# Four fused convolution layers with a woven state-space scan: the scan's inputs formed half a tile earlier, the products of the step preparation moved to other slots, the output sums two slots later

## The chip, the cores and the metric

One NeuronCore of a Trainium2 chip runs the whole program in one launch. The metric is device time in microseconds; three runs of the kernel before gave a median of 21075.38 us (21060.88 to 21089.58). A further run, taken with the hardware profiler, is the one that the profile and the trace describe: 21033.39 us, of which the instructions span 21031.6 us.

Engines are named as in the profile: PE is the matmul engine (PEld its weight loads), DVE the vector engine, ACT the scalar engine, POOL the GpSimd engine, SP the engine whose queue issues nearly all DMAs. Each works through its own list of instructions in the order in which the program gives them; semaphores hold an instruction until what it reads or overwrites is ready.

## The reference, cut to what matters

```python
# x: (4, 128, 128, 128) float32
x = x + _L0_conv_ref(_gn(x), ...)   # deformable 3x3 convolution (bilinear gathers)
x = x + _L1_conv_ref(_gn(x), ...)   # dilated 5x7 convolution and two 1x1 layers
x = x + _L2_conv_ref(_gn(x), ...)   # layer norm, depthwise convolutions, state-space scan, gate, layer norm
x = x + _L3_conv_ref(_gn(x), ...)   # 3x3 convolution and a Laplacian of the channel sum
```

The change lies in the scan of layer 2, which runs in four directions k over every image (by rows and by columns, each forwards and backwards):

```python
dts = einsum('bkrl,kdr->bkdl', dts, dt_w)
A = -exp(A_logs).reshape(K, C, 16)
delta = softplus(dts + dt_b[None, :, :, None])
def step(h, inp):
    u, d, b, c = inp                       # one position l
    dA = exp(d[..., None] * A)
    h = h * dA + (d * u)[..., None] * b[:, :, None, :]
    y = einsum('bkcn,bkn->bkc', h, c)
    return (h, y)
```

So each of 128 channels carries 16 states; each state is decayed by exp(delta·A), gets delta·u·B as its input, and the 16 states weighted by C are summed into y.

## The kernel before

**Blocks, tiles, slots.** `scan` works through 512 blocks: 4 images, 4 directions in the order k = 0, 1, 3, 2, and 32 blocks of 512 positions each. k = 0 and 1 are forward blocks, 3 and 2 are backward ones (`back`). A block t has 16 slots n = 4·j + g, with j the tile and g the place in it. A tile is an array `h` of 128 partitions x 4 x 512, which holds 4 of the 16 states of every channel. In each slot DVE runs one `tensor_tensor_scan` over 512 positions (L1071), 8192 in all.

**What a tile needs.**
- `states_up(t, j)` (L925): a PE product of B and `u` into the PSUM bank `dub`.
- `inputs(t, j, engine)` (L931): `h = du * dub`, one instruction over 128 x 2048. On DVE it reads `dub` from PSUM. In plain blocks (below) the tile j = 3 is formed by POOL instead, from `bb`, which a DMA brings.
- `decay` (L952): ACT computes exp(delta·A) into a bank `pa`, one for each slot. There are two such banks, and a third (`bank(3)`) in the stretches where the work beside the scan leaves it free. `decays(at)` keeps the list one or two decays ahead of the scan.
- After its four scans, `carry_on` and `outputs` (L989, L996) save the last column and multiply `h` by C, on POOL in plain blocks and on DVE in the others; `sums` (L966) adds the four states on PE into the bank `yacc`, and `finish` (L981) copies that bank out when a block is complete.

**The preparation of a later block.** `prepare(t + 2)` (L854) is a generator, and a slot from 1 to 15 makes one step of it. It computes delta = softplus(...) and delta·u in these instructions: product `pdt` (L866), its two evictions `e` and `above` on ACT (L871, L873), `exp` (L875), 1 + e (L878), in forward blocks the product `pxbc` (L882) and its eviction `bc` (L888), `ln` (L884), a subtraction (L890), four products into `psum` (L898), the eviction `steps` (L904), and on POOL delta·u (L908). `spread_steps`, `spread_products`, `spread_inputs` and `spread_outputs` bring the results, spread over partitions, back by DMAs on SP's queue, one block before their use.

**One bank for four kinds of product.** `pdt`, `pxbc`, `psum` and `dub` all have `tag="dub"` in a pool with one buffer for it. So each such product waits until the reader of the one before it is done: ACT's evictions for the first three, DVE's `inputs` for `dub`.

**Two kinds of block.** While layer 0 of a later image runs beside the scan, its gathers keep POOL busy; `c["by"]` is then DVE, and DVE does all four `inputs` and all `outputs`. I call these gather blocks. The other blocks are plain: POOL does `outputs` and the fourth `inputs`.

**What sets the order.** `together` runs the scan as the main list and takes steps of the work beside it (the layers of the images before and after) after each slot, by a fixed share. `keep_order` then fixes each engine's list in the order of emission. So the program's text is the order, on each engine.

**The slots of the shared bank before.** In slot 2 stands `pdt`, in slot 3 `e` and `above` and then `states_up` of tile 1; at the start of slot 4 `inputs` of tile 1. In slot 6 stands `pxbc` (forward blocks), in slot 7 `bc` and then `states_up` of tile 2; at the start of slot 8 its `inputs`. In plain blocks `psum` stands in slot 11, `steps` in 13, the POOL product in 14 and `states_up` of the next block's tile 0 in 15; in gather blocks `psum` in 9, `steps` in 10, `states_up` of tile 3 in 11, and again the next tile 0 in 15. `sums` of tile j stands in the second slot of tile j + 2.

The loop's core, as it stands:

```python
if ("h", j) not in c:
    inputs(t, j, nc.vector)
...
if g == 3 and then[0] < len(seq) and not (then[1] == NG - 1 and c["by"] is nc.gpsimd):
    states_up(*then)
```

Of the kernel before, what the change touches and what calls it, by code (L numbers as in the profile page):

```python
# [10 lines left out]
F32 = mybir.dt.float32  # L11
# [101 lines left out]
def conv_preact_kernel(ctx: ExitStack, tc: tile.TileContext, a: dict, nb: int):  # L113
# [20 lines left out]
    def store(dst, src, after=3, of=None):  # L134

        waiting.append([after, of, dst, src])
# [61 lines left out]
    def slots(n):  # L198
        for _ in range(n):
            yield None  # L200
# [617 lines left out]
    def scan(pull):  # L818
# [34 lines left out]

        def prepare(t, early=False):  # L854
# [3 lines left out]
            if (st["b"], k) not in carries:  # L858
                carries[st["b"], k] = carry = small.tile([P, NST], F32, name="carry")
                nc.vector.memset(carry, 0.0)  # L860
            c["carry"] = carries[st["b"], k]
            c["bc"] = st["bc"][k % 2][i, k // 2]
            u = c["u"]
            yield
            pdt = pss.tile([P, N], F32, name="pdt", tag="dub")
            nc.tensor.matmul(pdt, wd[:, k, :], u, start=True, stop=True)  # L866
            yield

# [5 lines left out]
            yield  # L874
            nc.scalar.activation(e, e, AF.Exp, scale=-1.0)  # L875
            yield
            one_e = sp.tile([P, N], F32, name="one_e", bufs=1)
            nc.scalar.activation(one_e, e, AF.Identity, bias=1.0)  # L878
            yield
            if not back:  # L880
                px = pss.tile([P, N], F32, name="pxbc", tag="dub")
                nc.tensor.matmul(px, xbc[:, k, :], u, start=True, stop=True)  # L882
# [3 lines left out]
            if not back:  # L886
                bc = sp.tile([4 * NST, N], F32, name="bc", bufs=1)
                nc.scalar.copy(bc, px[0 : 4 * NST])  # L888
                store(st["bc"][k][i].rearrange("d j s t -> (d j s) t"), bc)
# [9 lines left out]
            yield  # L899
            if not early:  # L900
                yield
# [3 lines left out]
            yield  # L905
            if early:
                yield
# [17 lines left out]
        def states_up(t, j):  # L925

            c = blocks[t]
            c["pb", j] = p = pss.tile([P, N], F32, name="dub", tag="dub")
            nc.tensor.matmul(p, xb[:, seq[t][1], j, :], c["u"], start=True, stop=True)  # L929
# [59 lines left out]
        def carry_on(t, j, engine=nc.gpsimd):  # L989

            end = 0 if seq[t][3] else N - 1
            h = blocks[t]["h", j]
            copy = nc.scalar.copy if engine is nc.scalar else engine.tensor_copy
            copy(blocks[t]["carry"][:, j * NG : (j + 1) * NG].unsqueeze(2), h[:, :, end : end + 1])  # L994
# [21 lines left out]
        states_up(0, 0)  # L1016
        decays(-1)
        slots = len(seq) * NST
        for t, (st, k, i, back) in enumerate(seq):
            c = blocks[t]  # L1020
            carry = c["carry"]
            on_vector = beside.get("busy") == "POOL"
            c["by"] = nc.vector if on_vector else nc.gpsimd
            more = prepare(t + 2, on_vector) if t + 2 < len(seq) else iter(())
            if t > 0:
                fetch(t + 3)
            for j in range(NG):
# [3 lines left out]
                if ("h", j) not in c:  # L1031
                    inputs(t, j, nc.vector)
                h = c["h", j]
                if t + 1 < len(seq) and j in (1, 2):
                    spread_steps(t + 1, j - 1)
                at = t * NST + j * NG
                decays(at)
                if j == 1 and t + 1 < len(seq):
                    spread_inputs(t + 1)
                if j == 2 and t + 1 < len(seq):  # L1040
                    spread_outputs(t + 1)
                if j == 3 and back:
                    c["before"] = load(sp, blk(st["y"][k % 2], i), [P, N], "before", bufs=1)
                for g in range(NG):
                    n = j * NG + g
                    if g == 1:
                        decays(at + 1)
                        if t + 1 < len(seq) and j == 3:
                            spread_steps(t + 1, 2)
                            spread_steps(t + 1, 3)  # L1050
                        if t + 1 < len(seq) and j == (2 if c["by"] is nc.gpsimd else 3):
                            spread_products(t + 1)
                        next(more, None)
                        if before[0] >= 0:
# [16 lines left out]
                    nc.vector.tensor_tensor_scan(o, f, o, carry[:, n : n + 1], ALU.mult, ALU.add)  # L1071
# [430 lines left out]
```

## Time and profile before

| | us |
|---|---|
| median of 3 runs | 21075.38 |
| profiled run | 21033.39 |
| its span | 21031.6 |
| DVE busy | 16808.6 (80%) |
| PE busy | 16025.3 (76%) |
| POOL busy | 15945.9 (76%) |
| ACT busy | 13477.7 (64%) |
| 8192 scans on DVE (L1071) | 9967.9, mean 1.266 |
| 1625 `inputs` on DVE (L936) | 3697.9, mean 2.276, and 1455.8 idle before them |
| 1692 `outputs` on POOL (L1000) | 7666.8, mean 4.531 |
| 8192 decays on ACT (L963) | 5551.9, mean 0.686 |
| DMA engines, moved | 4641.27 MB, 221 GB/s |

"Busy" is the time in which an engine works on an instruction of the program. "Idle before" is the time in which an engine waited for an instruction of a group, and the name after `<-` is what ended the wait. Until about 2300 us the first image's layers run alone, and after about 20690 us the last image's layer 3; between them the scan runs. The gathers (L445) run beside it in three stretches, about 3300 to 5450, 8500 to 10600 and 13600 to 15500 us, each recognised by POOL's time in L445; by the place of the 356 `outputs` that DVE makes, about 92 of the 512 blocks are gather blocks or hold part of one, and 420 are plain. Between the starts of two blocks lie 29.9 us in plain and 63.0 us in gather blocks, on average.

### The profile page before, as it was taken

To read this page: it belongs to the slowest core of one execution; us is meant where nothing else is said; L and a number is where in the kernel's file an instruction comes from. 1 tells how busy PE (TensorE), PEld (TensorE's weight loads), DVE (VectorE), ACT (ScalarE), POOL (GpSimd) and SP (SyncE) were. 2 spreads that over 40 slices of the span, in tenths; PEclk is the share of its full clock that TensorE was granted. 3 is DMA by queue.
4 is the path that set the end of the run, shared out by engine and by line. 5 is a ranking of instruction groups with operands and counts; after the bars stand their busy time and mean duration, and the time that the engine had idled before them with its cause. 6 is when DMAs were issued, how large, how long until landed. Compare 5 with 4: busy or idle time off the path is not lost.

```text
span 21031.6 us, 207094 instructions
## 1 busy us (share of the span) xinstructions
PE 16025.3 (76%) x58778; PEld 6877.1 (33%) x58778; DVE 16808.6 (80%) x14665; ACT 13477.7 (64%) x26854; POOL 15945.9 (76%) x9469
## 2 busy tenths in 40 slices
PE   4667776777877788777787887877777877777778
PEld 2444222444322223344432222344432222222223
DVE  1222588888998899888899889978889888999983
ACT  3444676676667776566667775666666766655563
POOL 3664477666788888767768888867768889999994
PEclk7788887988988889889898998989988988789899
DMA  7666568777756777777776696777776677555673
GB/s 234 192 193 184 162 202 282 249 256 250 245 192 204 213 236 246 246 249 249 254 237 196 202 251 217 262 241 252 256 242 204 205 208 216 185 185 191 196 220 123
DMA packets 2869274, 4641.27 MB, mean 221 GB/s; under 512 B 1088976, under 2 KB 1361944, under 8 KB 2791200
## 3 DMA queue, kind: packets, MB, share of 16 engines
q1 hardware_dynamic: 2499488, 3419.78, 50.9%
q0 software_dynamic: 368640, 1208.25, 18.2%
q8 instruction: 470, 7.70, 0.1%
q14 instruction: 676, 5.54, 0.1%
HBM read 3682.39 MB, written 874.52 MB: 217 GB/s over the span
## 4 chain that ended last, share of the span: by engine, by line
PE 24%; DVE 22%; ACT 14%; issue 13%; POOL 11%; DMA 8%; another core or an unknown queue 6%; SPq 2%; DVEq 0%; POOLq 0%; ACTq 0%
DVE h L1071 12%; DVE h L936 8%; POOL h L1000 7%; PE pst L481 6%; ACT g L458 5%; PE dub L929 3%; PE psum L898 3%; ACT pa L963 3%; PE yacc L974 2%; DMA du<-stepsd 2%; DMA delta<-stepsd 2%; PE p L1297 2%; POOL h L936 2%; PE acc L496 2%
## 5 line engine op out<-in xcount | busy, mean ns | idle before, releaser
L1071 DVE TENSOR_TENSOR_SCAN h<-pa,carry,h 128x512 f32<-128x512 f32 x8192 | 9967.9, 1266 | 474.7 <-ACT pa L963 236.8
L963 ACT ACTIVATE pa<-delta,neg_a 128x512 f32<-128x512 f32 x8192 | 5551.9, 686 | 3911.7 <-DVE h L1071 3239.1
L1000 POOL TENSOR_TENSOR h<-h,cb 128x2048 f32<-128x2048 f32 x1692 | 7666.8, 4531 | 136.5 <-POOL carry L994 0.6
L445 POOL DMA_INDIRECT g<-table,idx x4608 | 4814.8, 1045 | 2317.7 <-issue 1477.3
L936 DVE TENSOR_TENSOR h<-du,dub 128x2048 f32<-128x2048 f32 x1625 | 3697.9, 2276 | 1455.8 <-PE dub L929 1000.3
L481 PE MATMUL pst<-ident,g 128*128 128x128 f32 x18432 | 2705.1, 309 | 1641.8 <-ACT smp L490 1015.5
L481 PEld LDWEIGHTS pst<-ident,g 128*128 128x128 f32 x18432 | 2449.0, 161 | 2537.7 <-ACT smp L490 1405.8
L929 PE MATMUL dub<-u,xb_sb 128*128 128x512 f32 x3250 | 2046.4, 715 | 1478.8 <-ACT above L873 960.5
L974 PE MATMUL yacc<-h,gather_sb 128*32 128x512 f32 x16384 | 2468.7, 677 | 868.9 <-POOL h L1000 609.6
L458 ACT ACTIVATE g<-g,wt 128x128 f32<-128x128 f32 x9216 | 2869.2, 392 | 58.6 <-DMA g<-table,idx 47.7
L490 ACT COPY smp<-pst 128x512 f32<-128x512 f32 x1152 | 668.3, 580 | 2104.0 <-remote 1637.9
L936 POOL TENSOR_TENSOR h<-du,bb 128x2048 f32<-128x2048 f32 x423 | 1925.2, 4551 | 16.8 <-DMA du<-stepsd 15.8
L471 DVE TENSOR_TENSOR g<-g,wl 128x512 f32<-128x512 f32 x2304 | 1484.1, 669 | 171.1 <-DMA g<-table,idx 151.2
L994 POOL COPY carry<-h 128x4 f32<-128x4 f32 x1692 | 332.0, 196 | 1535.8 <-DVE h L1071 1479.3
L929 PEld LDWEIGHTS dub<-u,xb_sb 128*128 128x128 f32 x3250 | 580.8, 212 | 2522.8 <-ACT above L873 1377.2
L496 PE MATMUL acc<-smp,w_sb 128*128 128x512 f32 x2304 | 1318.9, 656 | 49.4 <-DVE x L503 36.2
L1297 PE MATMUL p<-xn,w_l_sb 128*128 128x508 f32 (+2 forms) x2304 | 1198.4, 638 | 1.8 <-ACT xn L1276 1.8
L503 DVE TENSOR_TENSOR x<-acc,xres 128x512 f32<-128x512 f32 x128 | 87.7, 685 | 1351.7 <-remote 478.9
L974 PEld LDWEIGHTS yacc<-h,gather_sb 128*32 128x32 f32 x16384 | 343.9, 113 | 2445.9 <-POOL h L1000 1075.9
L908 POOL TENSOR_TENSOR steps<-steps,u 128x512 f32<-128x512 f32 x512 | 658.7, 1286 | 326.1 <-ACT steps L904 313.6
L866 PE MATMUL pdt<-u,wd 128*128 128x512 f32 x1024 | 635.6, 706 | 278.0 <-DVE h L936 266.2
L750 PE MATMUL px<-win,convw_sb 128*128 128x508 f32 (+1 forms) x1536 | 806.8, 623 | 26.9 <-DMA win<-win 24.0
(171 smaller groups left out, 17914.0 us busy)
## 6 DMA issues: line engine op xcount, KB each, us to landing
cb<-bcd SPq DMA_DIRECT2D x512, 1024.0 KB
delta<-stepsd SPq DMA_DIRECT2D x2048, 256.0 KB
du<-stepsd SPq DMA_DIRECT2D x2048, 256.0 KB
stepsd<-steps SPq DMA_DIRECT2D x512, 512.0 KB
table<-gt SPq DMA_DIRECT2D x512, 256.0 KB
bb<-bcd SPq DMA_DIRECT2D x512, 256.0 KB
g<-table,idx POOLq DMA_INDIRECT x4608
u<-urow SPq DMA_DIRECT2D x256, 256.0 KB
```

The lines of the kernel that those rows point to most:

```text
L445: nc.gpsimd.indirect_dma_start(out=g[:, r].rearrange("p q c -> p (q c)"), out_offset=None, in_=table, in_offset=bass.IndirectOffsetOnAxis( ...
L458: nc.scalar.activation(g[:, r, c, :], g[:, r, c, :], AF.Copy, scale=wv[:, 2 * h + r, q, k, c : c + 1])
L471: nc.vector.tensor_mul(g, g, wl.unsqueeze(3).to_broadcast([P, 2, 2, P]))
L481: nc.tensor.matmul(pst[:, r * P : (r + 1) * P], g[:, r % 2, q, :], ident, start=q == 0, stop=q == 3, is_transpose=True,)
L496: nc.tensor.matmul(got["a", i], w0[:, k, :], got.pop(("c", n)), start=k == 0, stop=k == KK - 1)
L929: nc.tensor.matmul(p, xb[:, seq[t][1], j, :], c["u"], start=True, stop=True)
L936: engine.tensor_mul(h, c["du"], b.unsqueeze(1).to_broadcast([P, NG, N]))
L963: nc.scalar.activation(pa, blocks[t]["d", g], AF.Exp, scale=neg_a[:, k, at : at + 1])
L974: nc.tensor.matmul(c["y"][g * Q : (g + 1) * Q, :], gather, c["h", j][:, g, :], start=j == 0, stop=last and not second,)
L1000: engine.tensor_mul(h, h, c["cb"][:, j, :].unsqueeze(1).to_broadcast([P, NG, N]))
L1071: nc.vector.tensor_tensor_scan(o, f, o, carry[:, n : n + 1], ALU.mult, ALU.add)
L1297: nc.tensor.matmul(dst, wt, src, start=n == 0, stop=n == len(jobs) - 1)
```

## The change

- `inputs` of a tile is formed before the scan of slot g = 2 of the tile ahead (for tile 0: of the block ahead), no longer at the start of its own tile. `states_up` for it moves from g = 3 to the end of g = 1.
- `prepare` starts with four empty steps and puts a product and its eviction into one step: `pdt`, `e` and `above` in slot 4; then exp, 1 + e and ln in slots 5, 6, 7; in slot 8 the subtraction, and in forward blocks `pxbc` and `bc`. In plain blocks `psum` comes in slot 9, `steps` in 11, the POOL product in 12; in gather blocks in 11, 12 and 13. A step is now made at the end of a slot, behind the scan.
- `sums` moves from g = 1 to g = 3, and `finish` of the block ahead from slot 7 to slot 9.
- `decays` is called alike in every slot. The spreads by DMA move by one slot or none: the third `spread_steps` from slot 13 to 12; `spread_products` from slot 9 to 8 in plain blocks, from 13 to 10 in gather blocks.
- The carry of a direction is made by `carry_of` when first asked for.

No arithmetic and no instruction is added or removed, and all pools keep their buffers. The generator `slots(n)` in the new text yields n times.

```diff
-        def prepare(t, early=False):
+        def carry_of(t):
 
             st, k, i, back = seq[t]
-            c = blocks[t]
             if (st["b"], k) not in carries:
...
+            return carries[st["b"], k]
+
+        def prepare(t, early=False):
+
+            st, k, i, back = seq[t]
+            c = blocks[t]
             c["bc"] = st["bc"][k % 2][i, k // 2]
             u = c["u"]
-            yield
+
+            def state_rows():
+                if back:
+                    return
+                px = pss.tile([P, N], F32, name="pxbc", tag="dub")
+                nc.tensor.matmul(px, xbc[:, k, :], u, start=True, stop=True)
+                bc = sp.tile([4 * NST, N], F32, name="bc", bufs=1)
+                nc.scalar.copy(bc, px[0 : 4 * NST])
+                store(st["bc"][k][i].rearrange("d j s t -> (d j s) t"), bc)
+
+            yield from slots(4)
             pdt = pss.tile([P, N], F32, name="pdt", tag="dub")
             nc.tensor.matmul(pdt, wd[:, k, :], u, start=True, stop=True)
-            yield
-
             dtb = col(V_DTB + k)
...
             nc.scalar.activation(one_e, one_e, AF.Identity, bias=minus)
-            yield
-            yield
-            if not early:
-                yield
-                yield
+            state_rows()
+            yield from slots(3 if early else 1)
             pd = pss.tile([P, N], F32, name="psum", tag="dub")
             for n, (t, sign) in enumerate(((e, ident), (one_e, less), (ln, ident), (above, ident))):
                 nc.tensor.matmul(pd, sign, t, start=n == 0, stop=n == 3)
-            yield
-            if not early:
-                yield
+            yield from slots(1 if early else 2)
             steps = sp.tile([P, 2, N], F32, name="steps", bufs=1)
             delta, du = steps[:, 0, :], steps[:, 1, :]
             nc.scalar.copy(delta, pd)
-            yield
-            if early:
-                yield
+            yield None
             nc.gpsimd.tensor_mul(du, delta, u)
...
+        inputs(0, 0, nc.vector)
         decays(-1)
...
-                if ("h", j) not in c:
-                    inputs(t, j, nc.vector)
+                up = then[0] < len(seq) and not (then[1] == NG - 1 and plain)
                 h = c["h", j]
-                if t + 1 < len(seq) and j in (1, 2):
-                    spread_steps(t + 1, j - 1)
                 at = t * NST + j * NG
-                decays(at)
-                if j == 1 and t + 1 < len(seq):
-                    spread_inputs(t + 1)
-                if j == 2 and t + 1 < len(seq):
-                    spread_outputs(t + 1)
...
+                    if g == 0:
+                        if coming and j:
+                            spread_steps(t + 1, j - 1)
+                        if coming and j == 1:
+                            spread_inputs(t + 1)
+                        if coming and j == 2:
+                            spread_outputs(t + 1)
+                            if plain:
+                                spread_products(t + 1)
                     if g == 1:
-                        decays(at + 1)
-                        if t + 1 < len(seq) and j == 3:
-                            spread_steps(t + 1, 2)
-                            spread_steps(t + 1, 3)
-                        if t + 1 < len(seq) and j == (2 if c["by"] is nc.gpsimd else 3):
-                            spread_products(t + 1)
-                        next(more, None)
                         if before[0] >= 0:
                             carry_on(*before, c["by"])
                             outputs(*before, c["by"])
-                        if earlier[0] >= 0:
-                            sums(*earlier)
-                    if n and g in (0, 3):
-                        next(more, None)
-                    if g == 3 and then[0] < len(seq) and not (then[1] == NG - 1 and c["by"] is nc.gpsimd):
-                        states_up(*then)
+                        if coming and j == 3:
+                            spread_steps(t + 1, 3)
                     if g == 2:
-                        decays(at + 2)
-                        if j == 0 and c["by"] is nc.gpsimd:
+                        if j == 0 and plain:
                             inputs(t, NG - 1, nc.gpsimd)
-                        next(more, None)
+                        if up:
+                            inputs(*then, nc.vector)
+                        if coming and j == 2 and not plain:
+                            spread_products(t + 1)
+                    decays(at + g)
                     o, f = h[:, g, :], c["a", n]
                     if back:
                         o, f = o[:, ::-1], f[:, ::-1]
                     nc.vector.tensor_tensor_scan(o, f, o, carry[:, n : n + 1], ALU.mult, ALU.add)
                     if g == 3:
                         decays(at + 3)
-                        if j == 1 and t > 0:
-                            finish(t - 1)
-                    yield (t * NST + n + 1) / slots
+                        if earlier[0] >= 0:
+                            sums(*earlier)
+                    if g == 1 and j == 2 and t > 0:
+                        finish(t - 1)
+                    next(more, None)
+                    if g == 1 and up:
+                        states_up(*then)
+                    yield (t * NST + n + 1) / total
```

More of the change, by code (lines that the diff above doesn't have):

```diff
@@ L852, in fetch @@
                 blocks[t]["u"] = load(sp, blk(us[k % 2], i), [P, N], "u", bufs=4)
+        def carry_of(t):
+            st, k, i, back = seq[t]
+            if (st["b"], k) not in carries:
+                carries[st["b"], k] = carry = small.tile([P, NST], F32, name="carry")
+                nc.vector.memset(carry, 0.0)
+            return carries[st["b"], k]
         def prepare(t, early=False):
@@ L857, in prepare @@
             c = blocks[t]
[L858 to L861, printed above, removed]
             c["bc"] = st["bc"][k % 2][i, k // 2]
             u = c["u"]
-            yield
+            def state_rows():
[7 more added lines that the diff above has]
+            yield from slots(4)
             pdt = pss.tile([P, N], F32, name="pdt", tag="dub")
             nc.tensor.matmul(pdt, wd[:, k, :], u, start=True, stop=True)
-            yield
             dtb = col(V_DTB + k)
@@ L873, in prepare @@
             nc.scalar.activation(above, pdt, AF.Relu, bias=dtb)
-            yield
+            yield None
             nc.scalar.activation(e, e, AF.Exp, scale=-1.0)
-            yield
+            yield None
             one_e = sp.tile([P, N], F32, name="one_e", bufs=1)
             nc.scalar.activation(one_e, e, AF.Identity, bias=1.0)
-            yield
-            if not back:
-                px = pss.tile([P, N], F32, name="pxbc", tag="dub")
-                nc.tensor.matmul(px, xbc[:, k, :], u, start=True, stop=True)
+            yield None
             ln = sp.tile([P, N], F32, name="ln", bufs=1)
             nc.scalar.activation(ln, one_e, AF.Ln)
-            yield
[L886 to L889, printed above, removed]
-            nc.scalar.activation(one_e, one_e, AF.Identity, bias=minus)
-            yield
-            yield
-            if not early:
-                yield
-                yield
+            yield None
+            nc.scalar.activation(one_e, one_e, AF.Identity, bias=minus)
+            state_rows()
+            yield from slots(3 if early else 1)
             pd = pss.tile([P, N], F32, name="psum", tag="dub")
@@ L898, in prepare @@
                 nc.tensor.matmul(pd, sign, t, start=n == 0, stop=n == 3)
-            yield
-            if not early:
-                yield
+            yield from slots(1 if early else 2)
             steps = sp.tile([P, 2, N], F32, name="steps", bufs=1)
@@ L904, in prepare @@
             nc.scalar.copy(delta, pd)
-            yield
-            if early:
-                yield
+            yield None
             nc.gpsimd.tensor_mul(du, delta, u)
@@ L993, in carry_on @@
             copy = nc.scalar.copy if engine is nc.scalar else engine.tensor_copy
-            copy(blocks[t]["carry"][:, j * NG : (j + 1) * NG].unsqueeze(2), h[:, :, end : end + 1])
+            copy(carry_of(t)[:, j * NG : (j + 1) * NG].unsqueeze(2), h[:, :, end : end + 1])
         def outputs(t, j, engine=nc.gpsimd):
@@ L1016, in scan @@
         states_up(0, 0)
+        inputs(0, 0, nc.vector)
         decays(-1)
-        slots = len(seq) * NST
+        total = len(seq) * NST
         for t, (st, k, i, back) in enumerate(seq):
             c = blocks[t]
[L1021 to L1024, printed above, removed]
+            carry = carry_of(t)
+            c["by"] = nc.vector if beside.get("busy") == "POOL" else nc.gpsimd
+            plain = c["by"] is nc.gpsimd
+            more = prepare(t + 2, not plain) if t + 2 < len(seq) else iter(())
+            coming = t + 1 < len(seq)
             if t > 0:
```

## The prediction, made before the changed kernel ran

> **What bounds the kernel now.** I read the page's busy times first, then the groups of instructions, then who waited for whom, then busy time by stretch, and last the timeline of one block.
>
> ```profile
> PE 16025.3 (76%) x58778; PEld 6877.1 (33%) x58778; DVE 16808.6 (80%) x14665; ACT 13477.7 (64%) x26854; POOL 15945.9 (76%) x9469
> ```
>
> No engine is full, so the path changes hands. By stretch (us of the stretch, then PE, PEld, DVE, ACT, POOL busy, granted clock, DMA share, GB/s), first plain blocks, then gather blocks, then plain blocks late in the run:
>
> ```profile
> 6000.00:8400.00 2400.00, 1929.68 (x5666) 646.96 (x5664) 2162.75 (x1673) 1685.26 (x2722) 2051.73 (x886) 0.90 0.71 219
> ...
> 8600.00:10500.00 1900.00, 1437.98 (x7237) 829.35 (x7236) 1532.51 (x1575) 1261.63 (x3256) 1355.30 (x1191) 0.89 0.75 248
> ...
> 18400.00:19900.00 1500.00, 1128.05 (x3512) 365.56 (x3504) 1463.48 (x1099) 871.01 (x1395) 1366.64 (x560) 0.90 0.57 189
> ```
>
> DVE leads in each: 90%, 81% and 98%. The last is the floor of a plain block: there the scan hardly waits. So what DVE loses elsewhere is what can be won. Two groups hold nearly all of the scan's losses (busy, mean ns, idle before, what ended it):
>
> ```profile
> L1071 DVE TENSOR_TENSOR_SCAN h<-pa,carry,h 128x512 f32<-128x512 f32 x8192 | 9967.9, 1266 | 474.7 <-ACT pa L963 236.8
> ...
> L936 DVE TENSOR_TENSOR h<-du,dub 128x2048 f32<-128x2048 f32 x1625 | 3697.9, 2276 | 1455.8 <-PE dub L929 1000.3
> ```
>
> The inputs lose three times what the scans lose, mostly to the product in the shared bank. Who waits for whom (total, times, longest):
>
> ```profile
> PE dub L929 <- ACT above L873: 960.5, 446, 11.0
> ...
> PE dub L929 <- ACT bc L888: 306.5, 184, 7.4
> ...
> ACT steps L904 <- PE psum L898: 153.5, 112, 12.8
> ACT e L871 <- PE pdt L866: 152.9, 67, 16.5
> ```
>
> PE stands at `dub` for ACT far longer than ACT stands for PE's `pdt`. One tile of a plain backward block shows the loop (start, duration, engine; in brackets the idle time):
>
> ```profile
> 6624.23 4.81 DVE L1071 TENSOR_TENSOR_SCAN h<-pa,carry,h 128x512 f32<-128x512 f32 x4
> ...
> 6625.55 0.69 ACT L963 ACTIVATE pa<-delta,neg_a 128x512 f32<-128x512 f32 x1 [0.81 <-DVE h L1071]
> 6625.92 1.02 PE L866 MATMUL pdt<-u,wd 128*128 128x512 f32 x2
> ...
> 6626.98 0.69 ACT L871 ACTIVATE e<-pdt,vec_sb 128x512 f32<-128x512 f32 x1 [0.74 <-PE pdt L866]
> 6627.57 0.68 ACT L873 ACTIVATE above<-pdt,vec_sb 128x512 f32<-128x512 f32 x1
> ...
> 6628.30 1.13 PE L929 MATMUL dub<-u,xb_sb 128*128 128x512 f32 x2 [0.51 <-ACT above L873]
> ...
> 6629.53 2.29 DVE L936 TENSOR_TENSOR h<-du,dub 128x2048 f32<-128x2048 f32 x1 [0.49 <-PE dub L929]
> ```
>
> A decay that follows a scan, then two evictions, then `dub`, then the input: the loop just misses the four scans that should cover it.
>
> I sorted the 1455.8 us before the inputs by tile. Plain blocks: tile 0 232, tile 1 374, tile 2 156 (122 of it in the 199 forward blocks, 0.61 each, against 0.15 in the 221 backward ones). Gather blocks: 199, 241, 154 and 101 for tiles 0 to 3; tile 2 has 2.02 a block forward (57) and 1.12 backward (35). So the waits sit where an eviction stands just ahead of `dub`: tile 1 behind `above` in every block, tile 2 behind `bc` in forward ones.
>
> **What the change does to each.** Counted from input to input, the lists keep their lengths: four scans still lie between tile 1's input and tile 2's, and the pair `pdt`, `above` still fits between, now ahead of tile 2. What moves is the slack. Today one slot lies between product and eviction and none between eviction and `dub`; afterwards it is the reverse.
>
> *Tile behind `above`.* Today the work beside the scan of one slot stands on ACT between the decay and `e`. Afterwards `e` may start when decay and `pdt` are both done. For each of 510 blocks I took from the trace the start of `e` less the later of those two ends, and took it off that block's wait: plain 370 falls to 249, gather 241 to 128. Gain 121 + 113 = 234.
>
> *Tile 2 behind `bc`.* Ahead of tile 1's `dub` stands nothing now but the block-ahead's input, three slots before; `pxbc` goes to the empty stretch behind the last input. I take the forward excess: 199 x (0.61 - 0.15) = 92 and 57 x (2.02 - 1.12) = 51. In gather blocks `bc` still precedes a `dub`, tile 3's, but with a slot between. Gain 143.
>
> *Tile 0.* `steps` to `dub` to input keep their distance of two slots, one slot and a half. Taken at 0; bounds: all 232 + 199 won, or as much again lost if `du` lands late. The DMAs that bring `du` may start when the third DVE input has read the old one, eight scans before the next input, before and after alike (in plain blocks 8 x 1.2 = 9.6 us, in which POOL's input, 4.55 us, is long done); today `DMA du<-stepsd` ends only 54.4 us of waits in all. SP passes no store or load on the way that it did not pass before: `spread_steps` and the 1 MB `cb` stand ahead of it in both orders.
>
> *`sums` two slots later.* POOL gets two more scans' time, and PE stands less before them: 609.6 us on POOL's `outputs`, 199.9 on `finish`. Behind the waiting sum now comes `pdt` or nothing urgent instead of `pdt` and `dub`. Bounds 0 and 100 (about a tenth of those waits reaching a `dub`); taken 50. In return an `h` tile lives four slots longer, at most five at once in plain blocks, which is all the pool has: tile 1's input then overwrites the tile whose sum stands one slot group earlier on PE, ahead of its own `dub`, so that wait is covered by the one for `dub`. If POOL lagged by more than four scans, 4.8 us, the cover would be gone and DVE would stand for POOL, which the 91% in the last stretch above does not suggest.
>
> *The order on ACT.* `e` stands directly behind `pdt`, `bc` behind `pxbc`. By the ends in the trace, `e` would stand 0.32 us a plain block and 1.36 a gather block, 134 + 125 = 259 against 169 today: 90 more. For `bc` I use the same means on the forward blocks: 199 x 0.32 + 57 x 1.36 = 141 against 58 today: 83 more. Behind them wait the decays, and with them the scans. ACT is 64% busy and two or three `pa` banks lie between, so I let a third reach DVE: 58; bounds 0 and 173.
>
> The Trainium skill (TensorE: Matmul & The Clock Gate, Architectural detail) says that ACT's queue is a strict first-in-first-out; by that rule alone all 173 would hold the decays behind, and the sum below would be 115 worse. The row that speaks for less is DVE's: of 3911.7 us that ACT idles before decays today, mostly by waiting for scans, scans lose only 236.8 to decays.
>
> *`steps` two slots behind `psum`, which now follows `bc`.* From the first `psum` product to the last end the trace has 3.6 us (10038.56 to 10042.15). On ACT between `bc` and `steps` stand three decays of 0.686 and the copy of `y`, 0.577: 2.6 us. So ACT must stand 1.0 us in a plain forward block, and decay 13 comes behind that. I let half reach DVE: 199 x 0.5 = 100; bounds 0 and 400 (2 us, if the work beside the scan delays `psum` too). The waits before slot 15 today, 97 us in plain blocks, move to slot 13 unchanged. In gather blocks product and copy keep their distance: 0.
>
> *Moves that cost nothing:* `carry_of`, `finish` two slots later (its only reader is `sums`, moved too), `decays` in one place, and POOL's delta·u, 1.286 us, which goes ahead of an `outputs` that waits for DVE anyway; without that wait it costs 1.3 us on POOL in blocks where POOL is full (17350 to 18400 us), as today.
>
> **Sum.** 234 + 143 + 50 - 58 - 100 = 269 us. From the profiled 21033 this makes 20764; the median of the runs shown lies 42 above the profiled run, so 20806 is the forecast, 1.3% faster. Its own range is 20560 to 20990.
>
> **Rivals.**
> - *ACT becomes the stall.* Place: slots 4, 8 and 11 of a block, where an eviction now stands directly or almost directly behind its product. If what ACT loses there, 173 + 400, reaches the scans whole, it takes back the 377 won at the tiles and 196 more; with a like delay in backward blocks (221 x 0.5) 306: 21270 to 21380. It decides once more than 0.74 us a block (377 / 512) shows up before the scans of slots 5 to 13. For it: in gather blocks `pdt` ends after the decay in more than half of the blocks. Against it: the two 152.9 and 153.5 above.
> - *The wait only moves.* The four scans still cover the same chain; tile 2 loses what tile 1 lost. Then 21030 to 21080. For it: the example above, where `e` waited for `pdt`, not for ACT. Against it: median 1.0 us between decay and `e` in plain blocks, 2.6 in gather blocks, of which little is `pdt`.
> - *The loop opens altogether.* With PE no longer standing 1267 us at `dub`, the waits of tiles 1 and 2, 925, go, and PE is ahead at tile 0 too: 20100 to 20250. Against it: POOL is 85 to 99% busy in plain blocks and takes over.
>
> **How the numbers follow.** Forecast 0.50, ACT stall 0.25, only moved 0.10, opened 0.15. The time is the forecast's, 20806 us. The range is 20350 to 21260: it cuts off half of the opened case and part of the stalled one. A difference of 0.2%, 42 us, is about what runs of this kernel can tell from none. Faster 0.65, within 0.2% 0.10, slower 0.25.
>
> **What would show it.** Right: idle before the DVE inputs falls from 1456 to about 1000; PE's waits for `above` and `bc` fall by more than half; DVE's share rises in plain blocks towards 93%; idle before the scans grows by less than 200. Wrong: idle before the scans, or ACT's before `e`, `bc` and `steps`, grows by more than the inputs lose; or new waits of DVE inputs for `du` or for POOL's `outputs`.

## The result and the profile after

The kernel after takes 21459.17 us (median of four runs, 21428.82 to 21488.88), the kernel before beside it 21079.62 (21060.88 to 21089.58): 1.0181 times as long, interval 1.0163 to 1.0199. It is slower, where the prediction had it 1.3% faster. The profiled run spans 21487.1 us. Its page, against that of before:

```profile
PE 16196.6 (75%) x58778; PEld 6929.2 (32%) x58778; DVE 16737.0 (78%) x14665; ACT 13455.7 (63%) x26854; POOL 15973.1 (74%) x9469
...
L1064 DVE TENSOR_TENSOR_SCAN h<-pa,carry,h 128x512 f32<-128x512 f32 x8192 | 9982.3, 1265 | 759.3 <-ACT pa L961 655.3
...
L934 DVE TENSOR_TENSOR h<-du,dub 128x2048 f32<-128x2048 f32 x1625 | 3697.3, 2275 | 1586.6 <-PE dub L927 859.6
```

The counts, and the means of DVE's two groups, are those of before; PE is busy 171 us longer, at a granted clock of 0.870 against 0.881, and waiting has grown. DVE idles 285 us more before the scans (474.7 to 759.3) and 131 more before the inputs (1455.8 to 1586.6). In the plain stretches DVE's share falls (columns as in the prediction):

```profile
6000.00:8400.00 2400.00, 1916.52 (x5522) 634.47 (x5522) 2133.67 (x1666) 1653.16 (x2678) 2023.50 (x876) 0.88 0.68 214
...
18400.00:19900.00 1500.00, 1136.14 (x3310) 354.57 (x3312) 1400.63 (x1062) 865.11 (x1391) 1342.26 (x561) 0.82 0.52 181
...
18750.00:20250.00 1500.00, 1159.49 (x3456) 369.82 (x3454) 1426.25 (x1079) 858.98 (x1371) 1345.20 (x550) 0.84 0.52 183
```

90% is now 89%. The 98% of the last stretch is 93%, and 95% in the third row, where the same blocks now stand some 380 us later: the scan waits there too. Who waits for whom (total, times, longest):

```profile
DVE h L1064 <- ACT pa L961: 655.3, 448, 17.3
PE dub L927 <- ACT above L885: 539.6, 373, 7.0
...
DVE h L934 <- DMA du<-stepsd: 309.1, 91, 26.3
ACT steps L904 <- PE psum L900: 300.5, 155, 17.7
PE psum L900 <- ACT bc L875: 248.1, 174, 7.6
PE psum L900 <- ACT one_e L895: 187.2, 119, 6.9
...
PE yacc L972 <- POOL h L998: 68.7, 63, 4.9
```

PE's wait for `above` is nearly halved (960.5 before), and that for `bc` ahead of `dub` fell from 306.5 to 12.2. But three waits are new or larger: DVE for `du` (54.4 before), PE at `psum` for ACT, and ACT at `steps` for `psum` (153.5 before).

By kind of block: a plain block takes 30.59 us (29.94 before), a gather block 64.95 (63.0). Idle time before the plain blocks' inputs, sorted by tile:

| | before | after |
|---|---|---|
| tile 0 | 232 | 604 |
| tile 1 | 374 | 29 |
| tile 2 | 156 | 270 |
| scans in slots 10 to 13 | 28 | 433 |

Tiles 1 and 2 won 231 us together, near the forecast (213). Tile 0, taken at nothing, lost 372. (The 232 include 29 us ahead of the very first block. In the kernel after that input still stands in slot 0, its 26 us are not in the 604, and counted alike tile 0 lost 398.) SP's queue shows what happens there (start, duration, queue). First before, with tile 2's input ended at 6612.31 and tile 0's begun, without a wait, at 6621.84:

```profile
6605.04 0.51 SPq L942 DMA_DIRECT2D bb<-bcd  x1
6605.65 0.56 SPq L916 DMA_DIRECT2D delta<-stepsd  x1
6606.26 0.59 SPq L948 DMA_DIRECT2D cb<-bcd  x1
6606.91 1.33 SPq L147 DMA_DIRECT2D win<-win  x2
6612.34 2.50 SPq L923 DMA_DIRECT2D du<-stepsd  x4
```

The old `du` is free at 6612.31 and the new one leaves 0.03 us later; `cb`'s megabyte left six microseconds earlier. Then after, in a block of the same direction, tile 2's input ended at 6623.10:

```profile
6608.97 0.53 SPq L914 DMA_DIRECT2D delta<-stepsd  x1
6620.33 0.52 SPq L940 DMA_DIRECT2D bb<-bcd  x1
6620.90 1.23 SPq L147 DMA_DIRECT2D win<-win  x2
6622.23 1.21 SPq L147 DMA_DIRECT2D yd<-yt  x2
6623.48 0.60 SPq L914 DMA_DIRECT2D delta<-stepsd  x1
6624.12 0.61 SPq L946 DMA_DIRECT2D cb<-bcd  x1
6624.83 3.25 SPq L921 DMA_DIRECT2D du<-stepsd  x4
...
6635.76 2.29 DVE L934 TENSOR_TENSOR h<-du,dub 128x2048 f32<-128x2048 f32 x1 [3.24 <-DMA du<-stepsd]
```

`bb` overwrites what POOL's input of tile 3 reads, and that input ended at 6620.30. SP sends nothing for 11 us, then four stores, `delta`, `cb` and `du` one behind the other; `du` starts 1.7 us after its buffer was free, right behind `cb`'s megabyte, and DVE stands 3.24 us. DVE's inputs moved two slots up; POOL's input, and with it `bb`, did not. Over the whole run SP stands longer at `bb`; the wait is put down to POOL's `carry`, the next entry of POOL's list behind that input. First before, then after:

```profile
SPq L942 <- POOL carry L994: 1542.6, 303, 10.1
```

```profile
SPq L940 <- POOL carry L992: 2643.8, 315, 18.0
```

Block by block, the traces show the same. In plain blocks POOL's input ends a median of 3.2 us ahead of tile 2's input on DVE, 8.1 before, and the gap between `cb`'s and `du`'s issue falls from a median of 5.2 us to 1.05. `du` leaves more than half a microsecond after its buffer is free in 158 of 419 plain blocks, 29 before; in 151 of the 158 SP issues everything from `bb` to `du` without a pause of half a microsecond. Of the waits of tile 0 that `du` ends, 271 us lie in these 158 blocks and 11 us in the others.

### The profile page after: what moved, and what is told of

Its sections match the earlier page's. It is cut to its first block, busy times and chain, and to the rows that moved or that the text cites. A ratio compares the mean times of both kernels' runs of the same rounds, so it can differ in the third digit from the quotient of the medians.

```text
span 21487.1 us, 206419 instructions
## 1 busy us (share of the span) xinstructions
PE 16196.6 (75%) x58778; PEld 6929.2 (32%) x58778; DVE 16737.0 (78%) x14665; ACT 13455.7 (63%) x26854; POOL 15973.1 (74%) x9469
## 4 chain that ended last, share of the span: by engine, by line
PE 26%; DVE 23%; ACT 17%; issue 11%; DMA 9%; another core or an unknown queue 8%; SPq 3%; POOL 3%; DVEq 0%; ACTq 0%; POOLq 0%
DVE h L1064 11%; DVE h L934 10%; ACT g L458 6%; DMA du<-stepsd 5%; PE psum L900 5%; PE pst L481 4%; ACT pa L961 3%; PE dub L927 3%; PE p L1295 2%; PE yacc L972 2%; PE pdt L880 2%; PE px L750 2%; SPq L921 1%; ACT smp L490 1%
## 5 line engine op out<-in xcount | busy, mean ns | idle before, releaser
L1064 DVE TENSOR_TENSOR_SCAN h<-pa,carry,h 128x512 f32<-128x512 f32 x8192 | 9982.3, 1265 | 759.3 <-ACT pa L961 655.3
L934 DVE TENSOR_TENSOR h<-du,dub 128x2048 f32<-128x2048 f32 x1625 | 3697.3, 2275 | 1586.6 <-PE dub L927 859.6
L927 PE MATMUL dub<-u,xb_sb 128*128 128x512 f32 x3250 | 2094.0, 731 | 1100.5 <-ACT above L885 539.6
L972 PE MATMUL yacc<-h,gather_sb 128*32 128x512 f32 x16384 | 2377.3, 653 | 84.5 <-POOL h L998 68.7
L880 PE MATMUL pdt<-u,wd 128*128 128x512 f32 x1024 | 773.4, 846 | 986.5 <-DVE h L934 985.0
```

The source lines that it names most:

```text
L934: engine.tensor_mul(h, c["du"], b.unsqueeze(1).to_broadcast([P, NG, N]))
L972: nc.tensor.matmul(c["y"][g * Q : (g + 1) * Q, :], gather, c["h", j][:, g, :], start=j == 0, stop=last and not second,)
```

## The experiments

Runs on two kinds of chip came up. On one the kernel before takes 21000 to 21080 us, on the other 20253 to 20268; there a gather block takes some 57.5 us instead of 63 to 65, and a plain block of the kernel after the same on both (30.55 to 30.60). So ratios are compared within a kind, and plain blocks across. The columns: ratio with its interval, us of a plain and of a gather block, idle before tile 0's input and before the scans of slots 10 to 13 in plain blocks. The kernel after stands in the first row; it, e1 to e4 and c1 to e11 ran on the slower kind. Where tile 0 stands in slot 0, 26 to 30 us of its wait are the first block's.

| kernel | ratio | plain | gather | tile 0 | slots 10-13 |
|---|---|---|---|---|---|
| after | 1.0181 [1.0163, 1.0199] | 30.59 | 64.95 | 604 | 433 |
| e1 products first | 1.0109 [1.0092, 1.0126] | 30.26 | 64.07 | 451 | 429 |
| e2 first tile back | 0.9995 [0.9986, 1.0005] | 29.70 | 64.06 | 93 | 458 |
| e3 wider chain | 1.0132 [1.0115, 1.0148] | 30.35 | 64.31 | 774 | 171 |
| e4 gather as before | 1.0110 [1.0093, 1.0127] | 30.55 | 62.82 | 581 | 446 |
| e5 sums as before | 1.0210 [1.0193, 1.0227] | 31.03 | 57.40 | 536 | 487 |
| e7 three undone | 0.9875 [0.9859, 0.9892] | 29.36 | 57.73 | 133 | 174 |
| e8 first tile kept | 1.0010 [1.0001, 1.0020] | 30.03 | 57.72 | 611 | 169 |
| e9 gather apart | 1.0104 [1.0088, 1.0121] | 30.56 | 57.39 | 595 | 435 |
| f1 gather heads | 1.0129 [1.0112, 1.0146] | 30.57 | 57.73 | 599 | 441 |
| c1 after again | 1.0174 [1.0157, 1.0191] | 30.55 | 63.98 | 588 | 439 |
| c2 gather as before | 1.0119 [1.0102, 1.0135] | 30.56 | 62.70 | 591 | 439 |
| e10 gather apart | 1.0174 [1.0157, 1.0191] | 30.56 | 63.94 | 591 | 446 |
| e11 apart and back | 0.9933 [0.9917, 0.9950] | 29.38 | 64.18 | 142 | 164 |
| f2 no cb | 1.0017 [1.0007, 1.0027] | 30.16 | 57.19 | 453 | 429 |
| f3 no cb, two du | 0.9986 [0.9976, 0.9996] | 30.03 | 57.14 | 353 | 454 |
| f4 three undone | 0.9873 [0.9856, 0.9889] | 29.36 | 57.76 | 132 | 177 |
| g1 after, third | 1.0109 [1.0092, 1.0126] | 30.60 | 57.30 | 603 | 439 |
| g2 gather heads | 1.0138 [1.0121, 1.0155] | 30.63 | 57.69 | 617 | 442 |

**The first tile.** e1 sends `du` ahead of `cb` in plain blocks, `cb` in slot 10:

```diff
                         if coming and j == 2:
-                            spread_outputs(t + 1)
                             if plain:
                                 spread_products(t + 1)
+                            else:
+                                spread_outputs(t + 1)
...
+                        if coming and j == 2 and plain:
+                            spread_outputs(t + 1)
```

> The kernel after, with one thing altered: in plain blocks the spread of du goes to SP ahead of slot 8's scan without the 1 MB spread of cb in front of it, and cb follows two slots later. Theory Q (in the kernel after, du leaves late because it stands behind cb on SP's queue): du is issued about 1.4 us earlier, the idle time before the inputs that is ended by du (309 us) falls below 100, tile 0's 604 us in plain blocks fall to about 350, and the time is 21180 to 21280. Rival P (the product dub of tile 0 is late at slot 13 anyway, since PE has stood at psum behind bc): the waits ended by du become waits ended by dub, tile 0 stays above 500, and the time stays within 60 of 21459.

```profile
DVE h L934 <- PE dub L927: 855.6, 532, 11.2
...
DVE h L934 <- DMA du<-stepsd: 109.7, 33, 26.5
```

The waits that `du` ends fall from 309.1 to 109.7, close to theory Q's mark of 100, but tile 0 only to 451, and those that `dub` ends stay (859.6 before this edit). Against the two runs of the kernel after on that kind of chip (1.0181 and c1's 1.0174) the ratio falls by 0.0065 to 0.0072, 137 to 151 us: Q is a part, and the rest of tile 0's wait ends with the product, as P has it.

e2 puts tile 0's input back to slot 0:

```diff
-                        if up:
+                        if up and (then[1] or not plain):
                             inputs(*then, nc.vector)
...
+                if ("h", j) not in c:
+                    inputs(t, j, nc.vector)
                 h = c["h", j]
```

> The kernel after, but in plain blocks the input of the next block's tile 0 stands again at the head of its block (slot 0) instead of slot 14; the rest stays. If the earlier place of tile 0's input is itself what the prediction missed, tile 0's wait falls from 604 back to some 230 us, while tiles 1 and 2 keep their 300, and the time is about 21459 - 372 = 21090. Rival P (PE and ACT are late in slots 9 to 13 and the input only shows it): the waits of the scans in slots 10 to 13 (434 us) stay, tile 0 keeps 450 or more, and the time stays above 21300.

```profile
L1066 DVE TENSOR_TENSOR_SCAN h<-pa,carry,h 128x512 f32<-128x512 f32 x8192 | 9995.8, 1266 | 878.7 <-ACT pa L961 723.3
...
L934 DVE TENSOR_TENSOR h<-du,dub 128x2048 f32<-128x2048 f32 x1625 | 3690.7, 2271 | 986.4 <-PE dub L927 600.4
```

This one change of place returns the whole loss: 0.0179 to 0.0186 less than the kernel after, 376 to 391 us. The inputs lose 986.4 us, about the 1000 that the prediction gave them, and tile 0 only 93: `du` now has ten scans to land in, not eight, and the product `dub` two more scans to be ready. So the run shows the place as the loss, but does not tell a late `du` from a late product. The scans lose even more than in the kernel after: what P names in slots 10 to 13 is a loss of its own.

f2 leaves out `cb`'s traffic, so that all outputs are multiplied by the first block's `cb` (the lines ahead of the first `...`); f3 also gives `du` two buffers and sends it in slot 4:

```diff
+            if t:
+                blocks[t]["cb"] = ahead["cb"]
+                return
-            blocks[t]["cb"] = p = bp.tile([P, NG, N], F32, name="cb")
+            blocks[t]["cb"] = ahead["cb"] = p = bp.tile([P, NG, N], F32, name="cb", bufs=1)
...
-            blocks[t]["du"] = p = sp.tile([P, NG, N], F32, name="du", bufs=1)
+            blocks[t]["du"] = p = sp.tile([P, NG, N], F32, name="du", bufs=2)
...
+                        if coming and j == 1 and plain:
+                            spread_products(t + 1)
```

> The kernel after with cb spread for the first block alone and read by all (the outputs are then multiplied by the first block's cb); du keeps its one buffer and its place. If du comes late because a megabyte of cb goes out in front of it, the waits before inputs that du ends fall from 309 below 80 and tile 0 from 604 below 400, like with du in front of cb (451). If the reuse of the one buffer is what binds (du leaves when tile 2's input has read the old one), they stay above 200.

> As the run before it, and du has two buffers and is sent in slot 4, ten slots before tile 0's input. Then du can't be late, and what is left before tile 0's input is PE's. If PE is late for its own reasons (psum, sums and background products ahead of dub in slots 9 to 13), tile 0 keeps 250 to 400 us. If PE's delay is itself fed by DVE's waits for du, tile 0 falls below 200. Either way it says how much of the 372 us lost at tile 0 no order on SP can win back.

Without `cb` tile 0 stands at 453, as with `du` ahead of it, and `du` still ends 122.7 us of waits, between f2's two marks (80 and 200): both `cb` and the one buffer count. With `du` never late (the 26.3 us left in f3 are one wait, before the first block) tile 0 stands at 353:

```profile
DVE h L934 <- PE dub L927: 664.0, 504, 11.2
...
DVE h L934 <- DMA du<-stepsd: 26.3, 1, 26.3
```

So of the 604 us some 150 are `cb`'s, 100 the single buffer's (with the later sending that it forces), and 353 stay with no `du` late, 317 of them ended by `dub`. In the trace of f3 PE comes to each of these late products straight from another product, without a pause: PE is behind with its list there. What put it behind was not separated. Before, `du` ended 54 of tile 0's 232 us, the first block's 29 among them, and others 178. Counted with the first block's 26 us, then, of the 398 lost some 223 are `du` (604 - 353 + 26 - 54) and 175 the rest (353 - 178), most of it the product.

**The chain.** e3 puts `pxbc` one slot ahead of `bc`, and `psum`, `steps` and POOL's product one slot later, in plain blocks (`state_product` holds the product, `state_rows` keeps `bc` and its store):

```diff
             nc.scalar.activation(ln, one_e, AF.Ln)
+            if not early:
+                state_product()
             yield None
...
-            yield from slots(3 if early else 1)
+            yield from slots(3 if early else 2)
```

> The kernel after, but in plain blocks pxbc goes to PE one slot before the copy bc instead of directly in front of it, and psum, steps and POOL's delta times u follow one slot later. Theory P (bc directly behind its product, then psum one slot behind bc, hold ACT and PE in slots 8 to 13): the plain scans' idle time in slots 10 to 13 falls from 434 to about 250 us, PE's wait of psum for bc (248 us) falls below 80, tile 0's wait falls by 100 or more, and the time is 21150 to 21250. Rival Q (du behind cb on SP): tile 0 stays at 550 or more and the time is 21380 or more.

```profile
L1073 DVE TENSOR_TENSOR_SCAN h<-pa,carry,h 128x512 f32<-128x512 f32 x8192 | 9964.2, 1264 | 437.8 <-ACT pa L970 334.7
...
L943 DVE TENSOR_TENSOR h<-du,dub 128x2048 f32<-128x2048 f32 x1625 | 3698.7, 2276 | 1775.1 <-PE dub L936 1017.1
```

The scans in slots 10 to 13 win 262 us, and tile 0 takes 170 of them back; 0.0042 to 0.0049, 88 to 103 us, stay. Both theories had half of it: the chain is a real loss, and behind it stands the next wait. `steps` now stands one slot nearer to tile 0's product. The run moves `pxbc` and `psum` together, so it does not say which of the two the gain belongs to.

e8 has e1, e3 and e4 together and keeps tile 0 in slot 14:

> The kernel after with tile 0's input kept in slot 14, but with what should make it possible: du ahead of cb on SP's queue, the wider chain in plain blocks, the loop of before in gather blocks. If tile 0's wait in slot 14 came from du's place behind cb and from the tight chain, tile 0 falls below 350 and the ratio is 0.995 or less. If the place itself is the loss (du can leave only when tile 2's input has read the old one, and needs as long as the eight scans take), tile 0 keeps 450 or more and the ratio is 0.998 to 1.006; it then lies 0.011 or more above the kernel with tile 0 back at slot 0.

Tile 0 still loses 611. Against e7, whose plain blocks differ in tile 0's place and the order of `du` and `cb`, a plain block takes 0.67 us more, 281 us over 420: the place is the loss. But `du` is not the greater part of it here: by the trace `dub` ends 462 of the 611 us and `du` 136. With the wider chain, tile 0's product is the tighter one.

**The sums.** e5 puts `sums` back to g = 1 and `finish` to slot 7.

> The kernel after with sums and finish back at their old slots (1, 5, 9, 13 and 7), nothing else altered. If the later sums bring the 50 us that the prediction gave them (POOL's outputs have more time: PE's wait of sums for POOL fell from 609.6 to 68.7), this kernel is 50 us or more slower than the kernel after, ratio 1.0205 or more. If the sums in slot 11 are what makes PE late for tile 0's product (63 us of its waits end behind sums, 49 times), it is faster: ratio 1.015 or less, and tile 0 falls below 540. If neither reaches DVE, the ratio stays at 1.018.

```profile
PE yacc L972 <- POOL h L998: 1179.9, 512, 5.7
```

Against e9, on the same chip and with the new sums, a plain block takes 0.47 us more, 197 us over 420. With the inputs earlier, PE would wait for POOL's `outputs` 1179.9 us; with the sums later it is 68.7. Tile 0 does fall to 536, just under the second theory's mark, but tile 1 rises from 30 to 110 and tile 2 from 265 to 383. This part of the change is a gain, four times the 50 us of the prediction.

**Gather blocks.** e4 and c2 give them the loop and preparation of before; e9 and e10 only put `pdt` and `pxbc` one slot ahead of their evictions; f1 and g2 only put their inputs back to the head of the tile (with `psum` one slot later and `du` behind the last input).

> The 92 gather blocks run the loop and the preparation of the kernel before (inputs at the head of their tile, product and eviction one slot apart, sums at slot 1), the plain blocks those of the kernel after. If the new order itself costs the gather blocks their 1.96 us each, they are back at 63.0 us a block and the time is about 21459 - 180 = 21280. If the gather blocks lost only because gathered rows or the plain blocks around them come otherwise, they stay near 65 us and the time is 21420 or more.

> The kernel after, unaltered, once more on one chip beside the next three. In the first set of runs (kernel before 21021) a gather block took 63 to 65 us, in the second (kernel before 20268) 57.4 to 57.7, whatever the kernel, while a plain block of the kernel after took 30.6 in both. Theory G (evictions directly behind their products cost the gather blocks 1.96 us each wherever they run): the ratio is 1.018 and a gather block here takes 2 us more than with the loop of before beside it. Rival W (they cost only where gathered rows come slowly): where the kernel before takes about 20270, the ratio is 1.010 and gather blocks take 57.4; where it takes about 21020, 1.018 and 65.

> The kernel after with the gather blocks in the loop of before, as in the fourth run, now on the same chip as the unaltered one. Theory G: ratio 1.011, 0.007 below the kernel after. Rival W: on a chip where the kernel before takes about 20270, within 0.002 of the kernel after; where it takes about 21020, 0.007 below it.

> The kernel after, but in gather blocks pdt goes to PE one slot ahead of e and pxbc one slot ahead of bc, the rest of the gather blocks and all plain blocks unchanged. If evictions directly behind their products cost the gather blocks their 1.96 us (ACT's wait at e 169 to 308 us, the scans' at a decay 137 to 302), their scans' idle time falls from 302 to 200 or less, a gather block to 64.0 us or less, and the ratio to 1.014 or less. If it is the place of inputs and outputs among the scans (the bare scans around them wait: slots 0, 1, 4, 5, 8, 9, 12, 13), the scans keep 270 or more and the ratio is 1.0165 to 1.0195.

> In gather blocks pdt one slot ahead of e and pxbc one slot ahead of bc, the rest as after; the ninth run again, now beside the unaltered kernel. Where the unaltered kernel's gather blocks take 2 us more than those with the loop of before, they come back to within 0.5 us of these if the order of product and eviction is the cause, and stay 1.5 us above if the place of inputs and outputs is. Where the unaltered kernel's gather blocks lose nothing, all three are within 0.5 us.

> The kernel after, but in gather blocks the inputs stand again at the head of their tile (slots 0, 4, 8, 12, their products in slot 2 of the tile before, psum one slot later, du behind the last input); evictions stay directly behind their products and sums in their new slots. If the place of the inputs (two scans before and two after, so that a decay bank must be had right after an input and an output) costs the gather blocks, they come back from 64 to 62.7 us and the ratio, where the kernel before takes about 21000, is 1.010 to 1.013. If it is the order on ACT or the later sums, they stay at 63.8 us or more and the ratio at 1.016 to 1.019.

> The kernel after, unaltered, beside the next. Where the kernel before takes about 21000, ratio 1.017 to 1.019 and a gather block of 64 to 65 us; where it takes about 20260, 1.010 to 1.012 and 57.4 us, since there only the plain blocks lose.

> Inputs of the gather blocks at the head of their tile, the rest as after, once more. Where the kernel before takes about 21000: 62.7 us a gather block and a ratio 0.005 or more below the unaltered kernel if the place of the inputs costs the gather blocks, 63.8 us or more and within 0.002 of it if not. Where it takes about 20260, 57.7 us and 0.001 to 0.003 above it.

On the slower kind of chip the old loop wins 0.0055 to 0.0071; product ahead of eviction wins nothing (63.94 against 63.98 us), so that reading of ACT's waits falls. The ratio of e9 seemed to speak for it, but on the faster kind the kernel after stands at 1.0109 by itself, so rival W holds: there gather blocks lose nothing (57.30 against 57.7 with inputs at the head). f1 and g2 both fell on that kind. What costs the gather blocks on the slower kind, the place of inputs and outputs or the sums, stays open.

**A version that beats both.** e7 and f4 have e2, e3 and e4 together; e11 has e2 and, in all blocks, `pdt` and `pxbc` one slot ahead of their evictions (with it e3's slots for `psum` and `steps`).

> The kernel after with three things altered at once, in plain blocks tile 0's input at the head of its block and the wider chain (pxbc one slot ahead of bc, psum and steps one slot later), in gather blocks the loop of before. What is left of the change is the move of tiles 1 and 2 and of the sums in plain blocks. Alone, the three gave 1.86%, 0.49% and 0.71% of the 1.81% lost. If they are independent losses, they add up: ratio 0.987, and with slot 13's waits (270 us with tile 0 back) now won whole, because slot 14 no longer takes them back, down to 0.980. If they are one loss in three places, the ratio stays between 0.995 and 1.0.

> The version with three parts undone once more: tile 0 back at slot 0 and the wider chain in plain blocks, the loop of before in gather blocks. If the losses are independent on this chip too, ratio 0.984 to 0.990; a plain block takes 29.4 us, a gather block 62.7.

> A version meant to beat both: the kernel after with tile 0's input at slot 0 in plain blocks, and in all blocks pdt and pxbc one slot ahead of their evictions, in plain blocks psum and steps one slot later. The kernel with the three parts undone stood at 0.9875. If pdt directly in front of e also holds ACT in plain blocks (its waits of e for pdt and for gathered rows were 308 us), the ratio is 0.980 to 0.987; if e one slot later only brings back tile 1's and 2's wait behind above, it is 0.988 to 0.995.

The inputs in e7:

```profile
L997 DVE TENSOR_TENSOR h<-du,dub 128x2048 f32<-128x2048 f32 x1625 | 3689.7, 2271 | 555.1 <-PE dub L990 432.1
```

The two runs of the first stand at 0.9875 and 0.9873 on the faster kind; on the slower kind e11, whose gather blocks are those of the new order, at 0.9933. A plain block takes 29.36 and 29.38 us in them, so `pdt` one slot ahead of `e` is worth nothing there. e7's 0.987 was forecast from three parts, taken off the 1.0181 of the slower kind. On the faster kind the third part is worth nothing (57.73 us a gather block against g1's 57.30) and the start is 1.0109, so that the forecast number was partly luck. But 1.0109 less what e2 and e3 won (0.0179 to 0.0186 and 0.0042 to 0.0049) is 0.9874 to 0.9888: the two parts in plain blocks add up. What is left of the change, tiles 1 and 2 and the sums, is 0.58 us a plain block better than before, 244 us.

## Why the prediction was wrong

- **Tile 0: the step that failed.** "Taken at 0", because `steps`, `dub` and input keep their distance, because `du` may leave when the third DVE input has read the old one, "before and after alike", and because "SP passes no store or load on the way that it did not pass before". The order on SP was indeed kept, and POOL's input was done ahead of tile 2's in all but one of 414 plain blocks. What was put at nothing is what that input holds up. `bb` waits for it at the head of SP's list; its lead over tile 2's input fell from 8.1 us to 3.2, since DVE's inputs moved up and it did not; and so `cb` and `du` leave back to back, and `du` late in 158 plain blocks instead of 29. In its place the runs showed a loss of 398 us at tile 0 in plain blocks: some 223 by `du`, 175 by the rest, mostly the product `dub`, whose distance in slots was kept and which PE reached late all the same. The bound that the step named, as much lost as there was to win, would have held it (115 were won in gather blocks); the value 0 did not. e2 shows that this place alone is the difference between 1.018 and 1.000.
- **Tiles 1 and 2** in plain blocks: 231 us won, 213 forecast. The method, a block's wait less what `e` could start earlier, held: the tile behind `above` (tile 2 now) was given 249 us and lost 270, the other (tile 1) 64 and lost 29. PE's wait for `bc` ahead of `dub` went (306.5 to 12.2); that for `above` fell by 44%, where more than half was named.
- **The same in gather blocks:** 164 us forecast at tiles 1 and 2, which lose 74 more instead (395 to 469). That all inputs together win 38 (695 to 657) is tile 0's 115, which the sum did not have. The scans of these blocks lose 155 more (147 to 302). So on this kind of chip the second rival, that the wait only moves, is nearer there; on the other kind gather blocks hardly wait at all (g1: 47 us before the inputs, 19 before the scans).
- **`sums`:** right in sign, 197 us instead of 50. The bound of a tenth was drawn from waits of the old order; with inputs earlier the old place would have cost more.
- **The order on ACT, 58 us:** nothing for `pdt` and `e`, nor for `pxbc` and `bc` in gather blocks; e10 and e11 move the product a slot ahead and win nothing. In plain forward blocks e3 and e11 move `pxbc` together with `psum`, so `bc`'s own part there is not shown. The rule of the Trainium skill that was weighed there (TensorE: Matmul & The Clock Gate, Architectural detail: ACT's queue is strictly first in, first out) would have made it dearer; what ACT stands at `e` didn't reach DVE in these runs.
- **`psum` and `steps`, 100 us:** 88 to 103 measured with tile 0 in slot 14 (e3), and 0.34 us a plain block, 143 us, with tile 0 back (e2 to e7), `pxbc`'s move included. Within its bounds.
- **The rivals.** The ACT stall came nearest, 21270 to 21380, and its mark was passed: plain scans in slots 5 to 13 lose some 373 us more, 0.89 us a block over the 420 plain blocks against the 0.74 named. But it is not what makes the kernel slower: e2 loses 481 us in those slots, the kernel after 453, and e2 stands level with before. That the stall's range lay closest to 21459 is in part luck: its own part, undone in e3, is 88 to 103 us, and its range holds no loss at tile 0. Of the marks named beforehand two came true: the scans' idle time grew by 285 us while the inputs won nothing, and DVE's inputs have new waits for `du`.

## What to carry to other kernels

When one engine's work is moved up, list what stays behind: another reader of the same buffers, the DMA that waits for that reader, and everything behind that DMA on its queue. A chain of last reader, transfer and next reader that just fits has no cover for a microsecond more. Undo each part of such a change alone before giving it up: here one part undone took the whole loss away, and three made it a gain of 1.25% on the faster kind of chip.

## What the runs showed of the hardware

Two kinds of chip were not expected. For the same kernel after, ACT's `smp` waits 1653.9 us, up to 40.5 at a time, for work without a name in the trace on the one (c1), and on the other (g1) that wait is not among the 190 largest; POOL's idle time ahead of its gathers, with nothing that the trace shows to end it, is 1421.6 us against 845.3, with a longest of 6.0 against 0.7:

```profile
ACT smp L490 <- remote: 1653.9, 346, 40.5
POOL g L445 <- issue: 1421.6, 3625, 6.0
```

```profile
POOL g L445 <- issue: 845.3, 2799, 0.7
```

The kernel before is 3.6 to 4.1% slower on the first, and the kernel after stands at 1.0174 to 1.0181 there, against 1.0109 on the second: a ratio from one chip doesn't carry over where a kernel gathers. What differs between the chips was not tried.
